# Moving the Newton step of an inverse norm, and the scaling by it, one piece later in an interleaved schedule

## The chip, the cores and the metric

The kernel runs on one core of a Trainium2 chip. The metric is the time of one execution on the device in microseconds (us), from the core's first to its last instruction. A core has five engines that work side by side, each through its own queue in the order in which the program was written: PE (TensorE, matrix products; PEld is its loading of weights), DVE (VectorE), ACT (ScalarE), POOL (GpSimd) and SP (SyncE, which issues the loads and stores here). They wait for one another by semaphores. Matrix products land in PSUM[...] .

## The reference, cut to what matters

Eight images of 256 channels by 2304 positions (48 x 48) go through two layers, each a group norm, a block and a residual sum. The first block clusters positions; only its beginning concerns the change:

```
feat_pos = tokens @ W.T + bias                     # (8, 2304, 512)
feat, pos = feat_pos[:, :, :256], feat_pos[:, :, 256:]
pos = pos / maximum(norm(pos, axis=-1), 1e-12)     # unit length for each position
sim = einsum('bnc,bmc->bnm', pos, pos)             # 2304 x 2304 for each image
topksim, topkid = top_k(sim, 16)
out = softmax(topksim) weighted sum of feat[topkid]
```

The second layer is two Mamba blocks in a row: a layer norm over the channels, a projection (`in_proj`), a short convolution (its taps), a projection to step sizes and to B and C, a scan along the 2304 positions with 16 states for each of 512 channels, a gate and a projection back.

## The kernel before, in words

**Two programs in one.** The top-k layer of image 0 runs alone at the start. After that the Mamba layer of image b and the top-k layer of image b + 1 are written into the same queues, so that one layer's work fills the other's gaps. `manual_schedule` keeps the order in which the Python code emits instructions.

**The scan loop** (from L955) sets the beat. It goes over half steps m; two of them, p = 0 and p = 1, make a step n of 32 channels by 4 states for each partition group. A half step has its exponentials on ScalarE (`decay`, L815), a scan on VectorE (`run_scan`, L830) and for about a third of the scans a product on VectorE (L832). At p = 0 GpSimd makes the input of the scan two steps ahead (`make_bx`, L791, called bx), multiplies the last step's states by C for the other scans (`pool_part`, L860) and, for the first chunk, sets a memory to zero (L803). The rest of the Mamba layer hangs on the half steps through the tables `between` and `behind`.

**The other layer** is a Python generator, `layer0` (L228). Each `yield` ends a *piece*. At the end of each half step the loop takes the next piece, and during the projections, until the generator has announced where its top-k rows begin, it takes two (L984 to L990).

**The projection stage** of `layer0` works on six chunks of 384 positions. `chunk` (L295) emits, a piece each: two products for pos (`project`, L302), three for feat (`features`, L311) and the sums of squares (`norms`, L321, named pn). Each product goes into a PSUM buffer named mm, of which the two layers together have three, and is taken out later: `step` (L235) keeps two products pending and takes out the older one (`leave_psum`) before it makes the next. Pos is taken out with its bias at L329 and squared at L336, feat is copied at L341, and the norms are copied at L346 into n2 (the profile's n).

**The inverse norm** of chunk c - 1 is made while chunk c is projected. `rsqrt_start` (L158) takes the logarithm and the exponential of -0.5 times it on ScalarE (L160, L161), which gives a rough 1/norm in rn. `rsqrt_end` (L163) makes one Newton step on GpSimd, five small instructions (L168 to L172: nv_rn, nt_rn, rn). `scale` (L284) spreads rn over the partitions with three small matrix products (`spread`, L218, named pb) into an mm buffer; its eviction, two steps later, is VectorE's product pos times pb (L289). In the kernel before, the exponential and the Newton step belong to the same piece as features 0; the spread is the next piece, ahead of features 1.

## Time and profile before

| | before |
|---|---|
| time, median of 3 | 10088.27 us (10084.85 to 10095.08) |
| span of the profiled execution | 10083.0 us |
| granted TensorE clock, mean | 0.883 |
| Newton instructions on GpSimd (L168 to L172) for rn | 5 x 48, 192 to 235 ns each |
| Ln, Exp for rn on ScalarE | 48 each, 288 and 204 ns |
| spread pb on PE, a product | 275 ns |
| scaling pos (L289) on VectorE | 48, 954 ns |

A row of the profile names the engine, the line of the kernel, the operation and its operands (written<-read, without buffer numbers), then how often or how long. In lists of instructions in order of time the first two columns are start and duration in us; a bracket at the end gives how long the engine had been idle before it and which instruction's end it was waiting for. In the lists of waits the columns are the total in us, how many times, and the longest.

### The profile page before, as it was taken

The page shows a single profiled execution, that of the slowest core. Times are in us where ns is not written, and L with a number is a line of the kernel's source. Part 1 is how long each engine was busy: PE and PEld are TensorE (multiplying, and loading weights), DVE is VectorE, ACT ScalarE, POOL GpSimd, SP SyncE. Part 2 cuts the span into 40 slices and gives each one's busy share as a digit, 9 for nine tenths or more (in the row PEclk, how much of TensorE's full clock was granted, in tenths as well). Part 3 has the DMA queues.
Part 4 walks back from the last instruction along what each step waited for, and adds up shares of the span by engine and source line. Part 5 has one row for each costly group of instructions (what it writes and reads, how often), then busy time and mean ns, then how long its engine had stood idle before and what let it go on. Part 6 is the DMA issues. An engine that isn't in the chain of part 4 may idle for free. (4 is left out here: it accounts for less than half of the span.)

```text
span 10083.0 us, 134837 instructions
## 1 busy us (share of the span) xinstructions
PE 8011.2 (79%) x36736; PEld 4387.2 (44%) x36736; DVE 8971.1 (89%) x7992; ACT 7487.2 (74%) x16998; POOL 8944.0 (89%) x3928
## 2 busy tenths in 40 slices
PE   8878886888868888688876888778886888866655
PEld 6544443444434444344443444344443444422222
DVE  4479998899979999799997999989998899988898
ACT  4477786778767777678776777777876778777776
POOL 0079998899989999799997999989998899999998
PEclk9989997899978999799988999889997899977777
DMA  1144444444444444444444444444445444444444
GB/s 31 34 126 122 137 128 144 118 133 124 140 132 130 124 137 129 135 125 137 124 140 128 128 129 135 131 132 126 135 127 146 119 131 128 137 133 133 140 137 121
DMA packets 1243512, 1271.44 MB, mean 126 GB/s; under 512 B 266592, under 2 KB 1215840, under 8 KB 1242752
## 3 DMA queue, kind: packets, MB, share of 16 engines
q1 hardware_dynamic: 1230496, 1262.45, 43.8%
q8 instruction: 293, 4.80, 0.2%
q14 instruction: 467, 3.83, 0.1%
q10 hardware_dynamic: 12256, 0.36, 0.1%
HBM read 1048.94 MB, written 212.86 MB: 125 GB/s over the span
## 5 line engine op out<-in xcount | busy, mean ns | idle before, releaser
L791 POOL TENSOR_TENSOR bx<-BC,dtxr 128x1536 f32<-128x1536 f32 x1536 | 5301.9, 3455 | 81.4 <-PE y L878 37.8
L815 ACT ACTIVATE da<-dtr,A_sb 128x384 f32<-128x384 f32 x6144 | 3585.8, 584 | 817.3 <-DVE bx L830 626.6
L830 DVE TENSOR_TENSOR_SCAN bx<-da,bx 128x770 f32<-128x770 f32 x2040 | 3525.2, 1747 | 191.8 <-ACT da L815 142.3
L860 POOL TENSOR_TENSOR bx<-bx,BC 128x1536 f32<-128x1536 f32 (+1 forms) x1320 | 3306.5, 2505 | 253.2 <-DVE bx L830 235.7
L830 DVE TENSOR_TENSOR_SCAN da<-da,bx 128x770 f32<-128x770 f32 x1032 | 1810.9, 1755 | 247.0 <-ACT da L815 161.8
L591 PE MATMUL pe<-vn,inw 128*128 128x384 f32 (+1 forms) x3072 | 1244.9, 539 | 406.9 <-DVE xr L913 89.9
L391 PE MATMUL psim<-pos 128*128 128x512 f32 (+1 forms) x2880 | 1377.8, 611 | 203.0 <-ACT sim L400 88.5
L457 PE MATMUL po<-feat,aT 128*128 128x256 f32 x5184 | 1358.1, 411 | 21.2 <-ACT aT L446 14.9
L878 PE MATMUL y<-bx,sel 128*32 128x384 f32 x12288 | 1232.3, 537 | 40.3 <-POOL bx L860 30.6
L457 PEld LDWEIGHTS po<-feat,aT 128*128 128x128 f32 x5184 | 1027.3, 205 | 367.0 <-issue 112.1
L832 DVE TENSOR_TENSOR bx<-da,BC 128x768 f32<-128x768 f32 x1032 | 989.1, 958 | 35.5
L591 PEld LDWEIGHTS pe<-vn,inw 128*128 128x128 f32 x3072 | 585.7, 205 | 924.0 <-issue 212.1
L391 PEld LDWEIGHTS psim<-pos 128*128 128x128 f32 x2880 | 553.4, 206 | 837.9 <-issue 464.3
L878 PEld LDWEIGHTS y<-bx,sel 128*32 128x32 f32 x12288 | 398.1, 119 | 862.7 <-issue 735.5
L691 DVE SCALAR_TENSOR_TENSOR xc<-pe,cw,xc 128x384 f32<-128x384 f32 x1152 | 696.3, 611 | 37.6 <-ACT xc L683 10.4
L721 PE MATMUL pd<-dbl,dtp_sb 16*128 16x384 f32 x768 | 417.5, 658 | 340.9 <-ACT dt L730 171.2
L847 ACT COPY h_st<-da 128x2 f32<-128x2 f32 x832 | 131.6, 158 | 589.7 <-DVE bx L832 582.7
L437 PE MATMUL pt<-ident,sim 128*128 128x128 f32 x2592 | 533.3, 288 | 43.0 <-DVE v L655 18.5
L446 ACT ACTIVATE aT<-pt 128x512 f32<-128x512 f32 (+1 forms) x720 | 387.6, 547 | 230.1 <-PE pt L438 225.8
L896 PE MATMUL pw<-z,ow 128*128 128x384 f32 x1536 | 529.5, 497 | 21.0 <-DVE v L655 7.4
L429 ACT ACTIVATE rest<-left,three 128x512 bf16<-128x512 f32 (+1 forms) x720 | 467.0, 670 | 59.8 <-DVE left L414 59.8
L875 PE MATMUL y<-xc,dmat 128*128 128x384 f32 x768 | 391.7, 597 | 148.8 <-DVE xc L691 124.6
(148 smaller groups left out, 10057.2 us busy)
## 6 DMA issues: line engine op xcount, KB each, us to landing
dtxr<-dtx_d SPq DMA_DIRECT2D x6144, 48.0 KB, 1.8
dtr<-dt_d SPq DMA_DIRECT2D x6144, 48.0 KB, 1.8
BC<-bc_d SPq DMA_DIRECT2D x768, 192.0 KB, 3.7
inw<-in_in_wT_dram SPq DMA_DIRECT2D x768, 128.0 KB, 2.3
dtx_d<-dtx SPq DMA_DIRECT2D x384, 192.0 KB, 1.9
dt_d<-dt SPq DMA_DIRECT2D x384, 192.0 KB, 2.1
ow<-in_out_wT_dram SPq DMA_DIRECT2D x96, 512.0 KB, 4.1
dmat<-diag SPq DMA_DIRECT2D x384, 64.0 KB, 2.1
```

The lines of the kernel that those rows point to most:

```text
L391: nc.tensor.matmul(pm, pos[:, k, t * P : (t + 1) * P], pos[:, k, c0 : c0 + w], start=(k == 0), stop=(k == CB - 1),)
L437: nc.tensor.transpose(pt[:, q], row["sim"][:, r], ident)
L457: nc.tensor.matmul(row["po"], aT[:, m % PT, :], feat[:, m, :], start=(m == 0), stop=(m == NB - 1))
L591: nc.tensor.matmul(pe, w[:, k], unit["vn"][:, k, lo:], start=(k == 0), stop=(k == CB - 1))
L691: nc.vector.scalar_tensor_tensor(unit["xc"][e], unit["pe"][e][:, k : k + T], cw[:, unit["d"], e, k : k + 1], unit["xc"][e], ALU.mult, ALU.add,
L791: nc.gpsimd.tensor_tensor(bx[:, :, 1:], unit["BC"][0], unit["dtxr"][i // JR][:, i % JR : i % JR + 1, :].to_broadcast([P, Q, T]), ALU.mult,)
L815: nc.scalar.activation(da[:, s * (1 + T) + 1 : (s + 1) * (1 + T)], unit["dtr"][i // JR][:, i % JR, :], AF.Exp, scale=A_sb[:, unit["d"], i, ...
L830: nc.vector.tensor_tensor_scan(h, da, g, 0.0, ALU.mult, ALU.add)
L832: nc.vector.tensor_tensor(bx[:, :, 0:T], da.rearrange("p (q t) -> p q t", q=HQ)[:, :, 1:], unit["BC"][1][:, qs], ALU.mult,)
L860: nc.gpsimd.tensor_tensor(g[:, :, 0:T], g[:, :, 1:], unit["BC"][1][:, qs], ALU.mult)
L878: nc.tensor.matmul(y[j * G : (j + 1) * G, :], sel, unit["bx"][k * J + j][:, q, 0:T], start=False, stop=True, skip_group_check=True,)
L896: nc.tensor.matmul(pw, unit["ow"][:, k, cb * P : (cb + 1) * P], unit["z"][k], start=(k == 0), stop=(k == DB - 1),)
```

## The change

The Newton step leaves the piece of the exponential and becomes part of the next one, with features 1; the spread for the scaling comes one piece later still, after features 1 instead of before it. For the last chunk the exponential moves a piece ahead and the Newton step stays. It is for giving each engine a piece of other work between the links of the chain norms, exponential, Newton step, spread, scaling. The number of pieces is the same, and so is every instruction.

```
         def inverse_norm(c):
             rn[c] = small.tile([P, TB], F32, tag="rn", name=f"rn_{b}_{c}")
             rsqrt_start(rn[c], n2[c], tiny[:, 1:2])
+
+        def inverse_norm_end(c):
             rsqrt_end(nc.gpsimd, rn[c], n2[c], TINY, f"rn_{b}_{c}")
@@
             if c > 0:
                 inverse_norm(c - 1)
-            step(lambda: features(0), feature(0))
-            yield
-            if c > 0:
-                scale(c - 1)
-                yield
-            for j in range(1, TB):
+            for j in range(TB):
                 step(lambda: features(j), feature(j))
                 yield
+                if c > 0 and j == 0:
+                    inverse_norm_end(c - 1)
+                if c > 0 and j == 1:
+                    scale(c - 1)
+                    yield
             step(norms, norm)
@@
         leave_psum()
         leave_psum()
-        yield
         inverse_norm(NCH - 1)
+        yield
+        inverse_norm_end(NCH - 1)
         yield
         scale(NCH - 1)
```

In the order of the queues this means, for PE in chunks 1 to 5: before, features 0, spread of the chunk before, features 1, features 2, norms; after, features 0, features 1, spread, features 2, norms. Three mm buffers are shared, so the buffer that each product gets, and with it the eviction that it waits for, changes too.

More of the change, by code (lines that the diff above doesn't have):

```diff
@@ L371, in layer0 @@
         leave_psum()
+        inverse_norm(NCH - 1)
         yield
-        inverse_norm(NCH - 1)
+        inverse_norm_end(NCH - 1)
         yield
```

## The prediction

> **What bounds the kernel now.** I read the page's first part, then the busy time by stretch, then the chain of waits of GpSimd and VectorE, then the instructions in order of time around the changed pieces.

> ```profile
> PE 8011.2 (79%) x36736; PEld 4387.2 (44%) x36736; DVE 8971.1 (89%) x7992; ACT 7487.2 (74%) x16998; POOL 8944.0 (89%) x3928
> ```

> VectorE (DVE) and GpSimd (POOL) share the lead at 89%, but that is an average over stages. The two stretches below are of one image's turn. The first is the projection stage, which the change edits; the second is the top-k stage after it. The columns are PE, PEld, DVE, ACT and POOL busy us, then the granted clock, the DMA share and GB/s.

> ```profile
> 1740.00:1855.00 115.00, 98.95 (x411) 60.65 (x412) 78.61 (x74) 85.15 (x198) 74.24 (x78) 0.84 0.37 103
> ...
> 2050.00:2300.00 250.00, 216.88 (x1039) 122.09 (x1038) 236.21 (x210) 196.35 (x444) 241.30 (x101) 0.95 0.45 128
> ```

> After the projections GpSimd is busy 241.30 of 250 us and VectorE 236.21, so time lost before that stretch is not won back there. In the projection stage both have slack (74 and 79 of 115) and PE, the fullest at 98.95, waits in turns with ScalarE and VectorE over three PSUM buffers: no engine is full, a ring of waits sets the pace. The stage runs seven times (images 1 to 7); each turn costs the same, so I follow that of image 2 and multiply.

> ```profile
> POOL nv_rn L168 <- ACT h_st L847: 113.8, 14, 10.3
> POOL nt_rn L169 <- ACT rn L161: 80.1, 48, 3.3
> POOL nv_rn L168 <- ACT n L346: 75.4, 31, 10.7
> ...
> DVE pos L289 <- PE pb L218: 118.1, 34, 14.2
> ```

> These are what the change aims at. GpSimd stands 269.3 us ahead of the Newton step (first, second and third line: waiting for the norms and for the exponential), VectorE 118.1 us ahead of the scaling. Of these, image 0's stage (30 to 90 us) has 35.8 + 5.0 and 45.0, where PE is busy 57.7 of 60 us and nobody's wait for the others costs anything. That leaves 228 us and 73 us, or 33 and 10 us an image, as the most that could be recovered: 3.0% in all if every microsecond were on the path.

> [...] So what counts is what stands behind a waiting one; the trace agrees (the bx product of GpSimd at 1788.40 starts only when the Newton step in front is through). [...] PE waited 1.24 us for pos (L289) before the second features of chunk 2. [...] the two exponential steps take 288 and 204 ns here, so [...] moving them is cheap.

> **The change, part by part.** No instruction is added or removed. While the projections run, two pieces are recorded in each half step of the scan loop, so "a piece later" is often no later for an engine whose big instructions come once in two half steps. The built order of the changed kernel shows what really moves.

> *Newton on GpSimd.* Of six Newton steps an image only that of chunk 1 (made in chunk 2) moves, behind one bx product (L791, 3.45 us), one L860 and a memset. The other five keep their neighbours, and their Ln and Exp keep their place on ScalarE except for the last chunk. So of 33 us an image, the chunk 1 wait is all that goes:

> ```profile
> 1786.80 0.20 POOL L168 TENSOR_SCALAR nv_rn<-n 128x3 f32<-128x3 f32 x1 [2.75 <-ACT n L346]
> 1787.36 0.19 POOL L169 TENSOR_TENSOR nt_rn<-rn 128x3 f32<-128x3 f32 x1 [0.36 <-ACT rn L161]
> ...
> 1788.40 3.45 POOL L791 TENSOR_TENSOR bx<-BC,dtxr 128x1536 f32<-128x1536 f32 x1
> ```

> GpSimd gains 2.75 + 0.36 = 3.1 us there. Its next Newton step waits for chunk 2's norms (0.66 + 2.89 us), which come from PE and ScalarE; it will wait 3 us longer there. Credit: 0.

> *Spread and scaling, chunk 1.* The order on PE was features 0, spread, in_proj, features 1 and 2, norms. It becomes features 0 and 1, in_proj, spread, features 2, norms. On VectorE the scaling moves behind one scan and one L832.

> ```profile
> 1779.07 0.56 DVE L884 TENSOR_TENSOR z<-y,z 128x384 f32<-128x384 f32 x1 [8.86 <-PE y L878]
> ...
> 1781.21 0.93 DVE L289 TENSOR_TENSOR pos<-pos,pb 128x768 f32<-128x768 f32 x1
> ...
> 1782.05 1.76 DVE L830 TENSOR_TENSOR_SCAN da<-da,bx 128x770 f32<-128x770 f32 x1
> ...
> 1783.45 1.48 PE L321 MATMUL pn<-ones_col,sq 128*128 128x1 f32 x12
> ...
> 1784.89 1.56 PE L302 MATMUL pp<-xt,w 128*128 128x384 f32 x4
> ```

> The spread's buffer is freed by the scaling. Before, features 2 took it, late enough to find it free; in the built order the norms (L321) take it and wait for VectorE. Scan ends 1781.29, the next scan 1783.0, L832 1784.0, scaling 1784.95: the norms start at 1785.0 and not at 1783.45, 1.5 us late. Behind them on PE stand the projection (1.56), an in_proj (1.57) and the second projection, which would begin at 85.0 + 1.45 + 1.55 + 1.5 = 1789.5. Before, it began at 1788.35, after 0.64 us of waiting for the taps (L691), and that wait hides 0.4. Net 1.1 us later on PE; ScalarE, which waited 1.11 us for that product, and its exponentials (L815) follow.

> *Chunk 2.* Two of three buffers are held by in_proj products until their taps. Features 1, spread, features 2 and norms pass one after another through the third, each after the eviction before it. The spread now comes behind the eviction of features 1, which on ScalarE stands behind two exponentials and two taps: scaling at about 1797 against 1792.85. VectorE runs 4 us late, but it has a wait to spend:

> ```profile
> 1807.14 1.28 ACT L697 ACT_TABLE_LOAD   x1
> ...
> 1809.66 0.95 DVE L289 TENSOR_TENSOR pos<-pos,pb 128x768 f32<-128x768 f32 x1 [4.16 <-PE pb L218]
> ...
> 1811.00 1.76 DVE L830 TENSOR_TENSOR_SCAN da<-da,bx 128x770 f32<-128x770 f32 x1
> ```

> That 4.16 us is in chunk 3, where the scaling also moves behind the scan. So VectorE is level again by then. What stays is one more eviction in the ring (the norms used to take a buffer freed by the taps): 0 if ScalarE is early, 1.5 us (the norms' own length on PE) if not. I take 0.4.

> *Chunks 3 and 5.* VectorE need not wait for the spread any more (4.16 and 4.40 us), so its scan comes 2 to 3 us sooner. In chunk 3 ScalarE's silu block (from the table load on) holds the next exponentials back; gain 0. In chunk 5 the eviction of features 1 moves ahead of an exponential pair and waits for its own product: the second product ends about 0.9 us after the first, so that pair, the dtr buffer that it frees and the BC load queued behind on SyncE come later. I take 0.7 (bounds 0 and 0.9). Chunk 4: order inside a half step only, 0.

> *Tail.* Ln and Exp of the last chunk move ahead of an exponential pair and the affine:

> ```profile
> 1845.39 0.26 ACT L346 ACTIVATE n<-pn,tiny 128x3 f32<-128x3 f32 x1 [0.92 <-PE pn L321]
> ...
> 1848.31 0.28 ACT L160 ACTIVATE rn<-n,tiny 128x3 f32<-128x3 f32 x1
> ...
> 1848.91 0.19 POOL L169 TENSOR_TENSOR nt_rn<-rn 128x3 f32<-128x3 f32 x1 [2.97 <-ACT rn L161]
> ...
> 1850.13 3.43 POOL L791 TENSOR_TENSOR bx<-BC,dtxr 128x1536 f32<-128x1536 f32 x1 [0.16 <-DMA BC<-bc_d]
> ```

> GpSimd loses its 2.97 us wait, but its next product then waits for the BC load, which landed at 1850.1. The 0.5 us of Ln and Exp now delays the affine that PE needs; 0.39 us of PE's wait for rn goes. Net +0.2.

> *Image 0.* PE is full in that stage and the work is the same: 0. Sum an image 1.1 + 0.4 + 0.7 + 0.2 = 2.4 us; times 7 = 17 us; 10088 + 17 = 10105.

> **The rivals.** *A, the waits were on the path, faster.* VectorE's sooner scans in chunks 3 and 5 (2.5 + 3.0 us) feed GpSimd, and nothing else holds: 7 x 5.5 = 38 us, 10050. For it: scans set the loop's pace, and GpSimd and VectorE are the busiest engines. Against: ScalarE, in one run of work from 1805 to 1823, does not wait for them. *B, the chunk 2 delay is not caught up, slower.* Of VectorE's 4 us some 3 stay beside the 2.4: 7 x 5.4 = 38 us, 10126. For it: PE ran slowly there (0.64 us a matmul against 0.39), so the walk may be too kind. Against: the 4.16 us wait. *C, no change*, 10088: the chunk 1 delay is absorbed as well, in waits such as the 1.98 us of ScalarE for pp in chunk 5.

> **How the numbers follow.** Forecast 0.50, A 0.20, B 0.23, C 0.07. The likeliest gives 10105. 0.2% is 20 us, so the borders are 10068 and 10108. The forecast's own spread (2.4 us an image, from 1.3 to 3.7 by the bounds above, so 10097 to 10114) lies above 10108 for a third: slower 0.17 + 0.23 = 0.40; same 0.33 + 0.07 = 0.40; faster 0.20. The range leaves out the deeper part of A and the end of B: 10062 to 10130.

> **What would show it.** Right: the waits of nv_rn and nt_rn together stay above 200 us; the wait of pos for pb falls from 118 to below 90; PE's norms (pn L321) gain a wait for pos L289, some 1.5 us seven times; in chunk 2 VectorE waits about 4 us for pb; the projection stage is 2 to 3 us longer and the top-k stage as long as before. Wrong: a stage that shrinks, with VectorE's scans of chunks 3 and 5 pulling ScalarE's exponentials forward (then A); or a delay of VectorE that lasts past chunk 3 (then B).

## The result and the profile after

The changed kernel takes 10130.31 us (median of 4, 10123.67 to 10135.13) against 10089.2 us (median of 4, 10084.85 to 10095.08): 1.0040 times the time before, 95% interval 1.0023 to 1.0057. It is slower, as forecast, but by 41 us and not by 17; the time lies at the very end of the range (10062 to 10130) and well above the forecast's own spread (10097 to 10114). The busy times are the same within 4 us. From the page of the changed kernel:

```profile
PE 8012.1 (79%) x36736; PEld 4387.2 (43%) x36736; DVE 8971.1 (89%) x7992; ACT 7491.2 (74%) x16998; POOL 8947.0 (88%) x3928
```

So the time is waiting, and nearly all of it lies in the projection stages. I measured each stage from the sixth scan of an image's turn to the 33rd: the seven add up to 773.2 us before and 813.0 us after, 5.7 us more for each. The rest changes by -5.1 us ahead of the first scan and +4.3 us everywhere else. The list of waits after, in answer to the four lines shown of before (us in total, times, longest):

```profile
POOL nv_rn L168 <- ACT n L348: 152.8, 29, 9.9
DVE pos L291 <- PE pb L218: 95.7, 27, 14.3
POOL nv_rn L168 <- ACT h_st L850: 66.1, 7, 10.0
POOL nt_rn L169 <- ACT rn L161: 60.6, 34, 3.9
...
PE pb L218 <- ACT feat L343: 12.6, 7, 1.8
...
PE pn L323 <- DVE pos L291: 8.8, 7, 1.3
```

The waits of the Newton step did not go: 279.5 us in all against 269.3. The wait of the scaling for the spread fell by 22 us, and PE got two new ones of seven each: the spread for the eviction of features 1 (1.80 us), and the norms for the scaling (1.26 us). Here are both in the turn of image 2: on PE the norms of chunk 1 and then chunk 2, and then VectorE:

```profile
1782.23 1.50 PE L323 MATMUL pn<-ones_col,sq 128*128 128x1 f32 x12 [1.25 <-DVE pos L291]
...
1789.25 1.03 PE L313 MATMUL pf<-w,xt 128*128 128x256 f32 x4
1790.12 1.54 PE L594 MATMUL pe<-vn,inw 128*128 128x387 f32 x4
1791.49 1.02 PE L313 MATMUL pf<-w,xt 128*128 128x256 f32 x4
1794.32 0.91 PE L218 MATMUL pb<-ident,rn 128*128 128x128 f32 x6 [1.80 <-ACT feat L343]
1796.27 1.13 PE L313 MATMUL pf<-w,xt 128*128 128x256 f32 x4 [1.04 <-DVE pos L291]
1797.86 1.50 PE L323 MATMUL pn<-ones_col,sq 128*128 128x1 f32 x12 [0.46 <-ACT feat L343]
```

```profile
1788.25 1.75 DVE L833 TENSOR_TENSOR_SCAN bx<-da,bx 128x770 f32<-128x770 f32 x1
1795.26 0.95 DVE L291 TENSOR_TENSOR pos<-pos,pb 128x768 f32<-128x768 f32 x1 [5.25 <-PE pb L218]
1796.13 1.75 DVE L833 TENSOR_TENSOR_SCAN bx<-da,bx 128x770 f32<-128x770 f32 x1
1797.80 3.73 DVE L694 SCALAR_TENSOR_TENSOR xc<-pe,cw,xc 128x384 f32<-128x384 f32 x6
...
1812.27 0.94 DVE L291 TENSOR_TENSOR pos<-pos,pb 128x768 f32<-128x768 f32 x1
```

VectorE stands 5.25 us for the spread of chunk 2 (5.3 us in six of the seven stages, 3.6 in the first), where it stood 0.23. Behind it in its queue are the six taps (L694) that free the two other PSUM buffers. The wait in chunk 3 that should have paid for this is gone (last line, no bracket), and still the stage is longer.

*The clock.* One thing is not in the list of waits. The traces record the clock granted to PE. In those of before and after it stands at 1.0 and at 0.5 by turns, and every stretch but the last, where the records end, is a multiple of 3.413 us (599 of 600 stretches before, 613 of 614 after). I cut three such windows around the wait of the norms in image 2's turn, first of before and then of after; the columns are PE, PEld, DVE, ACT and POOL busy us, and then the clock:

```profile
1782.13:1785.54 3.41, 3.41 (x21) 2.85 (x21) 3.38 (x4) 3.34 (x9) 1.91 (x3) 1.00 0.18 44
1785.54:1788.96 3.42, 3.09 (x9) 1.35 (x8) 3.35 (x5) 3.17 (x9) 1.55 (x6) 1.00 0.68 215
1788.96:1792.37 3.41, 3.41 (x15) 2.20 (x15) 3.38 (x3) 2.33 (x6) 3.41 (x2) 1.00 0.38 106
```

```profile
1780.69:1784.11 3.42, 2.17 (x16) 1.75 (x15) 3.42 (x4) 3.07 (x10) 3.42 (x3) 1.00 0.52 146
1784.11:1787.52 3.41, 3.41 (x7) 1.78 (x6) 3.30 (x5) 1.90 (x5) 3.08 (x7) 0.50 0.45 125
1787.52:1790.93 3.41, 3.41 (x13) 2.09 (x12) 2.48 (x2) 1.65 (x4) 3.33 (x3) 1.00 0.30 72
```

With the wait of 1.26 us a window is busy 2.17 of 3.42 us (0.63), and the next one runs at half clock, though PE is busy in all of it: 7 matmuls, where the window behind it has 13. This happens at the same place in the turns of images 2 to 7 after, and in none of before, where the window is 0.90 busy or more. A window at half clock costs up to half its length, 1.7 us of PE's work (an estimate from the 3.41 us at 0.50 above), more than the wait ahead of it.

### The profile page after: what moved, and what is told of

Read it like the earlier page. It is cut to its first block, busy times and chain, and to the rows that moved or that the text cites. A ratio compares the mean times of both kernels' runs of the same rounds, so it can differ in the third digit from the quotient of the medians.

```text
span 10122.0 us, 134844 instructions
## 1 busy us (share of the span) xinstructions
PE 8012.1 (79%) x36736; PEld 4387.2 (43%) x36736; DVE 8971.1 (89%) x7992; ACT 7491.2 (74%) x16998; POOL 8947.0 (88%) x3928
## 5 line engine op out<-in xcount | busy, mean ns | idle before, releaser
L694 DVE SCALAR_TENSOR_TENSOR xc<-pe,cw,xc 128x384 f32<-128x384 f32 x1152 | 695.9, 611 | 35.4 <-ACT xc L686 8.3
L878 PE MATMUL y<-xc,dmat 128*128 128x384 f32 x768 | 394.6, 601 | 144.8 <-DVE xc L694 117.9
```

What stands on the lines that cost most here:

```text
L694: nc.vector.scalar_tensor_tensor(unit["xc"][e], unit["pe"][e][:, k : k + T], cw[:, unit["d"], e, k : k + 1], unit["xc"][e], ALU.mult, ALU.add,
```

## The experiments

Each is timed in five rounds beside the kernel before; its ratio is to that kernel on the same chip (medians of 10091 to 10094 us in these sets). "Old" and "new" are the places before and after the change. In the diffs, the inner loop is that of a chunk's three features.

**The two halves of the change.** The scaling alone a piece later (Newton step and tail old), and the Newton step alone (scaling and tail old):

```
 e1   inverse_norm(c - 1); inverse_norm_end(c - 1)    # as before
      ...
-     if c > 0 and j == 0: scale(c - 1)
+     if c > 0 and j == 1: scale(c - 1)
 e2   if c > 0 and j == 0:
+         inverse_norm_end(c - 1)
          scale(c - 1)
```

> Spread and scaling a piece later in all chunks, Newton step and tail as before. Theory S (the scaling's new place in chunk 2, where VectorE waits 5.25 us for the spread, makes the loss): 10115 to 10132, nearly all of the changed kernel's 41 us. Theory N (the Newton step's new place on GpSimd makes it): 10088, no loss. Theory T (chunk 5 and the tail make it, +3.6 us an image there): half the loss at most, about 10100.

> Newton step a piece later in all chunks, spread, scaling and tail as before. Theory S: within 8 us of the kernel before (10088). Theory N: 10120 to 10132. Theory T: no change either.

Measured: 10126.03 us, 1.0035 (1.0022 to 1.0047), and 10093.55 us, 0.9999 (0.9990 to 1.0007). The Newton step's place is worth nothing either way; the scaling's makes the loss, 33 of the 41 us, and the other 8 are within the error of the two. e1 keeps the old tail, so the tail is small: the two half steps there (from the 27th scan to the 29th) take 7.4 to 7.7 us in e1 and 8.0 to 8.3 in the changed kernel, which is not told apart in the times.

**Chunk 2.** The changed kernel with chunk 2's scaling old, and the kernel before with chunk 2's scaling alone new:

```
 e3   if c > 0 and j == (1 if c != 2 else 0): scale(c - 1)   # rest as changed
 e4   if c > 0 and j == (1 if c == 2 else 0): scale(c - 1)   # rest as before
```

> The changed kernel with the scaling of chunk 2 alone back in its old place. Theory S: the 5.25 us wait in chunk 2 goes, 7 x 5 to 6 us, so 10088 to 10097. Theories N and T: less than 10 us won, 10120 or more.

> The kernel before with the scaling of chunk 2 alone a piece later. Theory S: 7 x 5 to 6 us lost unless the 4.16 us wait of chunk 3, which is still there, takes them up. With no catching up 10123 to 10130; with full catching up (the step of the forecast) 10090 to 10097. Theories N and T: 10088 to 10095.

Measured: e3 10116.72 us, 1.0026 (1.0016 to 1.0036); e4 10119.69 us, 1.0029 (1.0018 to 1.0041). Chunk 2 alone loses 26 us, 3.8 an image, near what no catching up gives. But taking it out of the changed kernel wins back only some 14 to 18, so my expectation for e3 failed: other chunks lose too. Whether the losses overlap (26 and 23 us against 41) is within the error. Why did the wait of chunk 3 not pay? The turn of image 6 shows it best, since chunk 1's norms start there at the same moment in both kernels (34.1 and 34.2 us into the stage). VectorE before, and then in e4:

```profile
6645.38 0.95 DVE L289 TENSOR_TENSOR pos<-pos,pb 128x768 f32<-128x768 f32 x1 [0.22 <-PE pb L218]
...
6660.50 0.95 DVE L289 TENSOR_TENSOR pos<-pos,pb 128x768 f32<-128x768 f32 x1 [3.33 <-PE pb L218]
```

```profile
6674.65 0.95 DVE L291 TENSOR_TENSOR pos<-pos,pb 128x768 f32<-128x768 f32 x1 [3.12 <-PE pb L218]
...
6690.14 0.95 DVE L291 TENSOR_TENSOR pos<-pos,pb 128x768 f32<-128x768 f32 x1 [4.07 <-PE pb L218]
```

There is a new wait of 3.12 us in chunk 2, and that of chunk 3 is longer, not shorter: 4.07 us for 3.33. Measured from the start of the stage, VectorE scales chunk 2 2.98 us later, and the spread of chunk 3 comes 3.35 us later. PE from chunk 2's norms to that spread, before and then in e4:

```profile
6649.88 1.50 PE L321 MATMUL pn<-ones_col,sq 128*128 128x1 f32 x12 [0.77 <-DVE xc L691]
6651.24 1.55 PE L591 MATMUL pe<-vn,inw 128*128 128x387 f32 x4
6652.63 2.74 PE L302 MATMUL pp<-xt,w 128*128 128x384 f32 x8
...
6659.63 0.83 PE L218 MATMUL pb<-ident,rn 128*128 128x128 f32 x6
```

```profile
6677.25 1.50 PE L323 MATMUL pn<-ones_col,sq 128*128 128x1 f32 x12 [0.46 <-ACT feat L343]
6679.16 1.90 PE L593 MATMUL pe<-vn,inw 128*128 128x387 f32 x4 [0.41 <-ACT n L348]
6680.86 4.14 PE L304 MATMUL pp<-xt,w 128*128 128x384 f32 x8
...
6689.27 0.83 PE L218 MATMUL pb<-ident,rn 128*128 128x128 f32 x6
```

PE works through this run in e4 with a single gap of 0.41 us, so every delay of the norms reaches the spread. The norms come only 1.08 us later; the other 2.27 us arise in the run itself (12.02 us for 9.75), where the eight projections meet the half clock (4.14 us for 2.74). In the seven turns the run takes 12.0 to 14.1 us in e4, each with a window or more at half clock; before, it takes 9.8 us in the three turns without one and 11.4 us in the four with one.

**Is it the third buffer?** The bank of po, a buffer in PSUM apart from mm, is used by the top-k stage alone. With the spread there, it leaves the ring of three mm buffers:

```
+    def po0(w, name):
+        return ps0.tile([P, 512], F32, tag="po", name=name, bufs=more)[:, :w]
-    step(lambda: spread(rn[c], TB, mm0, f"pb_{b}_{c}"), use)
+    step(lambda: spread(rn[c], TB, po0, f"pb_{b}_{c}"), use)
```

This was put into the changed kernel (e5) and into the kernel before (e6).

> The changed kernel, with the spread's product in the PSUM bank of po, which the projection stage does not use, in place of one of the three mm buffers. Theory R (the stall is the chain of features 1, spread, features 2 and norms through the third mm buffer): the spread of chunk 2 need not wait for features 1's eviction (1.80 us on PE), nor the norms of chunk 1 for the scaling; 3 to 5 us an image come back, so 10093 to 10108. Rival Q (the spread is late because of its place in the queue alone, behind features 1 on PE and behind ScalarE's exponentials through the Newton step): no gain, 10120 to 10132.

> The kernel before with the spread in the bank of po. Theory R: PE's wait for pos ahead of features 2 (1.05 us in chunk 2, 13.5 us in all while it stood for taps and scaling) goes, 0.5 to 2 us an image: 10078 to 10090. Rival Q: no change, 10088 to 10095.

Measured: e5 10099.44 us, 1.0004 (0.9996 to 1.0012); e6 10099.15 us, 1.0005 (0.9997 to 1.0014). All but 5 of the changed kernel's loss is gone, in the same order of instructions, and with that bank the new order (e5) and the old one (e6) take the same time: the order does harm through the buffers. In the turn of image 2 the spread of e5 starts right behind features 1, and VectorE waits 1.09 us in place of 5.25:

```profile
1790.45 1.02 PE L316 MATMUL pf<-w,xt 128*128 128x256 f32 x4
1791.32 0.83 PE L218 MATMUL pb<-ident,rn 128*128 128x128 f32 x6
```

```profile
1792.18 0.95 DVE L291 TENSOR_TENSOR pos<-pos,pb 128x768 f32<-128x768 f32 x1 [1.09 <-PE pb L218]
```

The second half of the theory failed: a fourth buffer is worth nothing to the kernel before. PE's wait for pos ahead of features (14.7 us in all before) goes there, but that of the norms for the taps grows from 5.3 to 11.2 us in all.

**The other chunks.** Chunk 1's scaling alone new (e7: `c == 1`), and those of chunks 3 and 5 (e8: `c in (3, 5)`).

> The kernel before with the scaling of chunk 1 alone a piece later. By the forecast's step (1.1 us an image): 10100. If the parts of scaling were additive (all of it 33 us, chunk 2 alone 26): 10095. If chunk 1 is what the changed kernel without chunk 2's part still lost (23 us, less 5 of chunk 5): 10110.

> The kernel before with the scaling of chunks 3 and 5 alone a piece later. By the forecast's step (chunk 3 nothing, chunk 5 0.7 us an image): 10098. If VectorE's earlier scans were worth something (rival A): 10060 to 10080. If chunks 3 and 5 make what was lost without chunk 2's part: 10112.

Measured: e7 10111.95 us, 1.0019 (1.0011 to 1.0027), 18 us or 2.5 an image; e8 10098.91 us, 1.0004 (0.9996 to 1.0012), some 0.65 an image and not told from nothing. Chunk 1 loses twice what the forecast gave it, and its loss appears in chunk 2: VectorE's wait for the spread grows from 118.1 to 134.6 us in all.

**Wait or clock?** Two kernels on top of e7. In e9 chunk 1's norms take the bank of po, so they no longer wait for the scaling. In e10 they still take the freed buffer, but PE is kept busy with products that nobody reads:

```
 e9   if c == 1: pn = ps0.tile([P, 512], F32, tag="po", ...)[:, :TB]
 e10  def fill(c, xn, n):                        # not for image 0
          idle = ps0.tile([P, 512], F32, tag="po", ...)[:, :T]
          for k in range(n):
              nc.tensor.matmul(idle, w0_sb[:, 0, C : C + P], xn[:, 0, :], ...)
      ...
+     fill(c, xn, {1: 3}.get(c, 0))
      step(norms, norm)
```

> The kernel with chunk 1's scaling alone a piece later (18 us lost), and chunk 1's norms in the PSUM bank of po, so that they don't wait for the buffer that the scaling frees. Theory W (the 1.25 us wait of the norms for pos on PE, and what follows from it, makes the whole loss): 10093 to 10098. Rival V (VectorE's later scaling itself, or ScalarE's new order, makes it): 10107 to 10113.

> The kernel with chunk 1's scaling alone a piece later, and three more matmuls (128x384, into the idle bank of po, read by nobody, about 1.2 us at full clock) on PE ahead of chunk 1's norms, in the 1.25 us in which PE stands. The wait stays as long; only PE is busy in it. Theory G (the window with that wait is 0.63 busy, which makes the next 3.4 us run at half clock, and that costs more than the wait): the dip some 37 us into the stage goes in images 1 to 6, and 10097 to 10104 is left of 10112. Rival D (the delay alone counts, the clock is chance): 10110 to 10116.

(The images 1 to 6 of this expectation are counted by the image in the scan; they are the turns of images 2 to 7.) Measured: e9 10092.01 us, 1.0001 (0.9993 to 1.0009); e10 10102.90 us, 1.0011 (1.0005 to 1.0018). The later scaling costs nothing once the norms don't wait for it. (e9 also takes one product out of the ring; in e6 that alone won nothing.) And with the fill some of the loss goes: 12 us are left of 18, each against its own set of times before (the intervals, 5 to 18 and 11 to 27 us, overlap). The norms even start later than in e7: the three products of 128x384 were six matmuls, not three, and took 2.10 us and not the 1.2 that I wrote. PE in e7 and then in e10, in the turn of image 5:

```profile
5438.20 1.03 PE L313 MATMUL pf<-w,xt 128*128 128x256 f32 x4
5440.48 1.60 PE L323 MATMUL pn<-ones_col,sq 128*128 128x1 f32 x12 [1.25 <-DVE pos L291]
5441.94 2.91 PE L304 MATMUL pp<-xt,w 128*128 128x384 f32 x4
5444.64 1.73 PE L593 MATMUL pe<-vn,inw 128*128 128x387 f32 x4
```

```profile
5425.79 1.03 PE L321 MATMUL pf<-w,xt 128*128 128x256 f32 x4
5426.66 2.10 PE L301 MATMUL fill<-xt,w 128*128 128x384 f32 x6
5428.59 1.40 PE L331 MATMUL pn<-ones_col,sq 128*128 128x1 f32 x12
5429.85 1.54 PE L312 MATMUL pp<-xt,w 128*128 128x384 f32 x4
5431.22 1.47 PE L602 MATMUL pe<-vn,inw 128*128 128x387 f32 x4
```

From the last features to the norms it is 2.28 us in e7 and 2.80 in e10 (0.87 in e9, where nothing waits), but the projection behind takes 1.54 us and not 2.91, since the clock holds:

```profile
5438.33:5441.74 3.41, 2.16 (x17) 1.71 (x15) 3.38 (x4) 3.31 (x9) 1.33 (x2) 1.00 0.38 102
5441.74:5445.16 3.42, 3.42 (x8) 2.03 (x8) 3.35 (x5) 1.09 (x5) 2.08 (x6) 0.50 0.57 167
```

```profile
5425.64:5429.05 3.41, 3.41 (x18) 2.51 (x18) 3.38 (x4) 3.31 (x9) 1.62 (x2) 1.00 0.00 0
5429.05:5432.46 3.41, 3.41 (x17) 2.40 (x17) 3.34 (x5) 2.13 (x7) 1.47 (x6) 1.00 0.60 174
```

What e10 still loses, 12 us or 1.7 an image, is about the delay of its norms, 2.80 - 0.87 = 1.93 us. The turns of e7 lean the same way: that of image 7, where the same wait was not followed by half clock, is 0.4 us longer than before, and those of images 2 to 6, where it was, are 2.0 to 7.0 us longer. But that of image 1, with a window at half clock too, is also 0.4 us longer, and equal turns of before differ by 3 us, so this is no proof.

**Filling elsewhere.** e11 is the changed kernel with such products in PE's waits of chunks 1 and 2 (`fill` of 3 and 1 ahead of the norms, 4 ahead of chunk 2's spread, 2 ahead of its features 2). e12 is the kernel before with one or so in each longer wait of the stage, meant to beat both.

> The changed kernel with such matmuls in PE's waits of chunk 1 (3 ahead of the norms) and chunk 2 (4 ahead of the spread, 2 ahead of features 2, 1 ahead of the norms). Theory G: both dips of these chunks go (at 37 and 52 us of the stage), 7 x 1.5 to 3 us: 10108 to 10120. Rival D: no gain, 10126 to 10136.

> The kernel before with matmuls that nobody reads in PE's waits of the projection stage: one product of 128x384 (two matmuls, 0.78 us at full clock) ahead of features 1 and of the norms of chunk 0, ahead of features 1 of chunk 2, and between the second and third step size product in chunk 4; six of 128x128 (1.6 us) in the 2.56 us wait ahead of the layer norm's mean. Theory G, if the half clock of this stage lies on the path as well in the kernel before: fewer windows at half clock and 2 to 4 us an image won, 10063 to 10077, faster than both kernels. If PE's clock doesn't bound the stage of the kernel before: 10088 to 10096. If the fill delays real work: 10097 or more.

Measured: e11 10120.18 us, 1.0029 (1.0018 to 1.0041); e12 10088.35 us, 0.9996 (0.9988 to 1.0005). In e11 no window from chunk 1's norms to chunk 3's spread is at half clock in any of the seven turns, and the time is 10 us below that of the changed kernel (their intervals overlap; in the traces the stages are 12.7 us shorter). The stretch of four scans in chunk 2 still takes 16.8 us (17.5 in six turns of the changed kernel, 11.7 before), so there the chain through the buffer counts and not the clock. Behind it the clock counts: from chunk 2's norms to chunk 3's spread it is 11.2 us in every turn of e11 and 12.9 in five turns of the changed kernel. In e12 the seven stages together spend 99 us at half clock and not 178, and no gain is measured. By the interval, a gain of some 12 us could be hidden, and what the added products delay was not measured apart. So most of this stage's half clock is not on the path of the kernel before, as far as e12 can tell. No version that I tried is faster than the kernel before.

## Why the prediction was right, and where its sizes were not

- *Newton step, credit 0*: right. e2 is 0.9999, and the waits of nv_rn and nt_rn stay above 200 us.
- *Chunk 1, 1.1 us an image*: the mechanism was right, the size was off. The norms wait 1.26 us for the scaling (1.5 forecast), and e9 shows that this wait, with what follows it, is the whole loss. But it measured 2.5 us. I took off 0.4 for 0.64 us of waiting for the taps. That was idle time of the weight loading (PEld): PE's in_proj ended at 1788.33 and the projection began at 1788.35, so PE had stood 0.02 us. (The 1.24 us "PE waited" ahead of chunk 2's second features is the weight loading's too; PE stood 1.05.) And I counted the wait once, without the half clock that follows the window with the wait. e10 speaks for that part: a longer delay without the half clock costs 12 us and not 18, though the intervals overlap.
- *Chunk 2, 0.4 us an image*: this step failed. VectorE is indeed late (5.25 us of waiting, about 4 forecast), through the chain features 1, spread, features 2, norms that I had described. What failed is "that 4.16 us is in chunk 3, ... so VectorE is level again by then". The wait was no slack: it was for PE, and PE carried the delay to chunk 3's spread, part of it by the later norms and more, in the turn of image 6, by the half clock behind them (e4). Alone the term measures 3.8 us. This is rival B's line, "some 3 stay", with its reason that the walk was too kind to PE. B's sign came too: in the turn of image 6 chunk 3's norms start 70.1 us into the stage and not 64.3.
- *Chunks 3 and 5, 0 and 0.7*: right within the error, e8 0.65 (interval -0.6 to 1.7). VectorE's earlier scans in chunk 3 are given back one scan later, so rival A fell here.
- *Tail, +0.2*: some 0.6 us in the traces, nothing that the times can tell.
- *Each turn costs the same*: it does not. Before, the seven took 109.3 to 112.5 us, and image 2's, from which the forecast was read, was among the longest (112.4 us, clock 0.86).
- *Image 0*: 5.1 us shorter to the first scan where 0 was forecast, in this pair of traces alone. In the stretch from 76 to 84 us, where the first similarity products stand, before and after:

```profile
76.00:84.00 8.00, 7.53 (x16) 3.99 (x17) 0.95 (x1) 0.85 (x2) 0.22 (x2) 0.61 0.00 1
```

```profile
76.00:84.00 8.00, 8.00 (x25) 4.12 (x26) 0.95 (x1) 2.10 (x4) 0.00 (x0) 1.00 0.00 1
```

The clock is 0.61 in one and 1.00 in the other. The first scan comes at 498.9 to 501.8 us in before, e6 and e12, where image 0's order is old, and at 496.7 to 502.2 in after, e1, e5 and e11, where its scaling is new, so this is no effect of the change that could be told.

The terms measured alone (2.5, 3.8 and 0.65 us) are 7 an image and the changed kernel loses 5.9 (3.3 to 8.2), which agrees within the error. That the range holds the time is luck: its end was drawn for rival B, which had 0.23, while the forecast's own path gave 10105, and "slower" had no more than 0.40. Of the signs named, the norms' wait, VectorE's wait in chunk 2, the waits for the Newton step and the unchanged top-k stage came as written; the wait of pos for pb fell to 95.7 and not below 90, and the stage grew by 5.7 us and not by 2 to 3, as the terms of chunks 1 and 2 were too small. That the rest of the losses in e3 splits between chunk 1, chunks 3 and 5 and the tail as these numbers suggest (18 and 5 us alone, 23 together) was not tried.

## What to carry to other kernels

Moving a product among others that rotate through a few PSUM buffers changes which eviction each of them waits for; write down the buffer of each product before and after, for that is where this change lost its time, and a fourth bank in the same order gave it back (e5, 1.0004 for 1.0040). A later engine's idle time pays for a delay only if what it waits for is not delayed by the same cause (in e4 the wait of 3.33 us grew to 4.07): follow the releaser back before you spend the wait. And count a new wait of PE with the half clock that may follow it (here 1.26 us of waiting, then 3.41 us at 0.50), but only where PE's products are on the path (in e12 99 us at half clock in place of 178 won nothing that was measured).
